# Group norm and attention over 48 x 48 images: VectorE's norm work queued instruction by instruction, another order at the start, and x buffers used for the last residuals

## The chip, the cores and the metric

The kernel runs on one core of one Trainium2 chip. The metric is the device time of one execution in microseconds (us), from ten runs of the kernel before. The engines are named as in the profile: PE (TensorE, matmuls), DVE (VectorE), ACT (ScalarE), POOL (GpSimd) and SP (SyncE, which here only issues transfers).

## The reference

Four images of 512 channels and 48 x 48 = 2304 positions ("tokens") go through a group norm, one matrix product to q, k and v, attention with 8 heads of 64 channels, and an output product that is added to the input.

```python
xr = x.reshape(b, 32, 16, h, w)                    # group norm: 32 groups of 16 channels
hn = ((xr - mean) * rsqrt(var + 1e-5)).reshape(b, c, h, w) * gn_scale + gn_bias
qkv = einsum('oc,bchw->bohw', qkv_w, hn) + qkv_b   # then cast to float16, split by head
w = softmax(einsum('bhct,bhcs->bhts', q * s, k * s))          # s = 64 ** -0.25
a = einsum('bhts,bhcs->bhct', w, v).astype(float32)
out = x + einsum('oc,bchw->bohw', proj_w, a) + proj_b
```

## The kernel before

**Tiling.** An image (a batch, b) is 512 x 2304 in channels x tokens: NC = 4 chunks of 128 channels (c), and NQ = 5 column blocks of tokens, four of 512 and one of 256 (j). So x of one batch is 20 tiles `x_b_c_j`, each with its own buffer, `x{c}_{j}`, reused from batch to batch; the norm is written over x in place. Heads are worked on in pairs, four per batch, sixteen in all (g).

**The stream.** The attention is a list of 432 *bursts*, 27 per head pair. A burst is three tiles of scores of 128 keys for both heads: six or more matmuls into PSUM (`scores`, L832), three exponentials on ACT from PSUM to an fp16 tile p (L839; three p buffers). One burst later VectorE adds p to the running sum over keys (`add`, L890, three folds at L893 at a block's end), two bursts later PE multiplies p by v into the one bank `av` (`values`, L857). At the end of a column block VectorE copies that bank out (avx, L866), and the same bank takes the sums over keys (`add_up`, sl, L910), which are copied out, sent to another layout by DMA, checked on POOL (L947), inverted on VectorE, sent through DRAM and back as a row over all partitions (ib, L966), and multiplied on POOL (att, L969).

**Fillers.** Everything else is cut into pieces in a list, `beside`, and issued between the bursts: the q and k products (`qk_chain`, L673, evacuated by VectorE at L682), the v product (`v_chain`, L713, L721), the output product (`proj_chain`, L761), whose input is converted by POOL to 32 bits (`att32`, L753) and whose result VectorE adds to a loaded piece of x (`residual`, three buffers; `proj_end`, L772), and the next batch's loads, statistics (bn_stats, L590), group mean and variance (two small matmuls, L597 and L607, with small VectorE steps and one POOL power for rstd, L615) and norm (L629). In each burst `fill` takes pieces from the head of the list as long as a credit in us allows; a piece can carry a `gap`, the least number of bursts since the last issued piece. Each run of `stats` issues four VectorE instructions (one per chunk) together, `norm` four, `group_mean` eight.

**What sets the order.** For PE and DVE the order of instructions is the order in which the code emits them. ACT, POOL and SP are placed by a scheduler. `chain_bank` gives fillers one PSUM bank at a time; the scores have three (`ps_s`), av and sl share one.

**Start and end.** At the start the x tiles of batch 0 are loaded block by block over two queues (SP and ACT), with q, k and v weights behind them; bv is spread over the partitions by POOL (`partition_broadcast`, L530); then all 20 statistics, mean, variance, and per block the norm and two chains. At the end the projection of the last batch's blocks 3 and 4 follows the last burst, and a flag (a count of sums in range, one small matmul) decides whether a general path is taken.

Of the kernel before, what the change touches and what calls it, by code (L numbers as in the profile page):

```python
# [25 lines left out]
P = 128  # L26
# [5 lines left out]
BURST = 3  # L32
# [434 lines left out]
def fast_path(  # L467
# [30 lines left out]
    def load_x(b, j, engines):  # L498

        o, n = QBLOCKS[j]  # L500
        for c in range(NC):
            t = xpool.tile([P, n], F32, tag=f"x{c}_{j}", name=f"x_{b}_{c}_{j}")
            engines[c % len(engines)].dma_start(t, x[b, bass.ts(c, P), o : o + n])
            hn[b, c, j] = t

    for j in range(NQ):
        load_x(0, j, (nc.sync, nc.scalar))
# [6 lines left out]
    brow = work.tile([1, C], F32, tag="avx", name="brow")  # L514
# [3 lines left out]
    nc.gpsimd.dma_start(bproj, proj_b)  # L518
    nc.gpsimd.dma_start(
# [3 lines left out]
    for part, engine in ((1, nc.sync), (0, nc.scalar), (2, nc.sync)):  # L523
        cols = bass.ts(part, C)
        engine.dma_start(
            wqkv[:, :, cols], qkv_wT[:, cols].rearrange("(c p) o -> p c o", p=P)
        )

    bv = const.tile([P, C], F32, name="bv")
    nc.gpsimd.partition_broadcast(bv, brow[0:1, :], P)  # L530
# [52 lines left out]
    st, mvs, coef = {}, {}, {}  # L583

    def stats(b, j):

        if j == 0:
            st[b] = small.tile([P, NC, NQ, 6], F32, tag="st", bufs=1, name=f"st_{b}")
        for c in range(NC):
            nc.vector.bn_stats(st[b][:, c, j, :], hn[b, c, j])  # L590

    def group_mean(b):
        mv = small.tile([P, NC, 2], F32, tag="mv", name=f"mv_{b}")
        for c in range(NC):
            nc.vector.bn_aggr(mv[:, c, :], st[b][:, c].rearrange("p j s -> p (j s)"))
        pm = chain_bank(f"gmean_{b}")[:, :NC]
        nc.tensor.matmul(pm, gmat2, mv[:, :, 0], start=True, stop=True)  # L597
        mean = small.tile([P, NC], F32, tag="gmean", name=f"mean_{b}")
        nc.vector.tensor_copy(mean, pm)
        dev = small.tile([P, NC], F32, tag="gdev", name=f"dev_{b}")  # L600
        nc.vector.tensor_tensor(dev, mv[:, :, 0], mean, ALU.subtract)
        dev2 = small.tile([P, NC], F32, tag="gdev2", name=f"dev2_{b}")
        nc.vector.tensor_tensor(dev2, dev, dev, ALU.mult)
        var = small.tile([P, NC], F32, tag="gvar", name=f"var_{b}")
        nc.vector.tensor_tensor(var, mv[:, :, 1], dev2, ALU.add)
        mvs[b] = mean, var

    def group_var(b):
        mean, var = mvs.pop(b)
        pv = chain_bank(f"gvar_{b}")[:, :NC]  # L610
        nc.tensor.matmul(pv, gmat2, var, start=True, stop=True)
        veps = small.tile([P, NC], F32, tag="veps", name=f"veps_{b}")
        nc.vector.tensor_scalar(veps, pv, EPS, None, ALU.add)
        rstd = small.tile([P, NC], F32, tag="rstd", name=f"rstd_{b}")
        nc.gpsimd.tensor_tensor(rstd, veps, mhalf, ALU.pow)  # L615
        ga = small.tile([P, NC], F32, tag="ga", name=f"ga_{b}")
        nc.vector.tensor_tensor(ga, rstd, gsc, ALU.mult)
        mga = small.tile([P, NC], F32, tag="mga", name=f"mga_{b}")
        nc.vector.tensor_tensor(mga, mean, ga, ALU.mult)
        gb = small.tile([P, NC], F32, tag="gb", name=f"gb_{b}")  # L620
        nc.vector.tensor_tensor(gb, gbi, mga, ALU.subtract)
        coef[b] = ga, gb

    def norm(b, j):

        ga, gb = coef[b]
        for c in range(NC):
            t = hn[b, c, j]
            nc.vector.tensor_scalar(  # L629
                t, t, ga[:, c : c + 1], gb[:, c : c + 1], ALU.mult, ALU.add  # L630
            )
# [5 lines left out]
    def piece(us, run, first=False, last=False, gap=0):  # L637
        return [us, run, first, last, gap, 0, NG]
# [20 lines left out]
    def qk_chain(g, part, j):  # L659
        b, pr = divmod(g, NPAIR)  # L660
        o, n = QBLOCKS[j]
        pw = {}

        def one(c):
# [4 lines left out]
            if c == 0:  # L669
# [557 lines left out]
```

## Time and profile before

| | |
|---|---|
| median of 10 runs | 1686.3 us (1684.07 to 1693.47) |
| profiled execution | 1691.31 us, its span 1689.5 us |
| mean granted PE clock | 0.987 |
| PE busy | 1602.8 us, 95% of the span |
| VectorE busy | 1135.1 us, 67% |
| ACT busy | 1232.6 us, 73% |
| POOL busy | 361.0 us, 21% |
| PE busy from 0 to 92 us | 65.8 us |
| PE busy from 1600 to 1690 us | 67.4 us |

The profile is of one execution. Its page gives busy time by engine, the span in 40 slices of 42.2 us (each digit the busy share in tenths, PEclk the granted clock), and the costliest groups of instructions. In the list of waits a row names the waiting instruction, the engine and instruction that released it, and after the colon the total us, how often, and the longest. In the order of time a row gives the start, the duration, the engine, the line, the operation with output <- input, and in brackets how long the engine had been idle and what ended that. In the view by windows a row gives a stretch in us, its length, the busy us of PE, PE's weight loads, DVE, ACT and POOL with their instruction counts, the granted clock, the DMA share and GB/s.

### The profile page before, as it was taken

The page shows a single profiled execution, that of the slowest core. Times are in us where ns is not written, and L with a number is a line of the kernel's source. Part 1 is how long each engine was busy: PE and PEld are TensorE (multiplying, and loading weights), DVE is VectorE, ACT ScalarE, POOL GpSimd, SP SyncE. Part 2 cuts the span into 40 slices and gives each one's busy share as a digit, 9 for nine tenths or more (in the row PEclk, how much of TensorE's full clock was granted, in tenths as well). Part 3 has the DMA queues.
Part 4 walks back from the last instruction along what each step waited for, and adds up shares of the span by engine and source line. Part 5 has one row for each costly group of instructions (what it writes and reads, how often), then busy time and mean ns, then how long its engine had stood idle before and what let it go on. Part 6 is the DMA issues. An engine that isn't in the chain of part 4 may idle for free.

```text
span 1689.5 us, 28311 instructions
## 1 busy us (share of the span) xinstructions
PE 1602.8 (95%) x11504; PEld 701.5 (42%) x11504; DVE 1135.1 (67%) x1280; ACT 1232.6 (73%) x1297; POOL 361.0 (21%) x497
## 2 busy tenths in 40 slices
PE   3999999799999999989999999999999999999795
PEld 1533454244333443445333344444533334444344
DVE  5257666876666667777666666877766666676764
ACT  0068787777887887767777877776777888877980
POOL 1002212112211211232221121133211121223331
PEclk9999999899999999999999999999999999999998
DMA  6001002200000113530200001442010000034243
GB/s 206 1 13 26 17 15 65 71 14 17 14 11 14 17 24 98 126 101 17 48 14 11 14 17 40 102 126 79 20 45 11 14 17 14 14 91 117 57 113 108
DMA packets 93772, 81.84 MB, mean 48 GB/s; under 512 B 50880, under 2 KB 58944, under 8 KB 93632
## 3 DMA queue, kind: packets, MB, share of 16 engines
q1 hardware_dynamic: 91488, 76.51, 17.3%
q10 hardware_dynamic: 1968, 3.41, 0.6%
q8 instruction: 92, 1.51, 0.4%
q14 instruction: 48, 0.39, 0.1%
q0 software_dynamic: 176, 0.02, 0.0%
HBM read 60.44 MB, written 19.16 MB: 47 GB/s over the span
## 4 chain that ended last, share of the span: by engine, by line
PE 85%; DVE 6%; DMA 3%; ACT 3%; issue 2%; POOL 0%; SPq 0%; ACTq 0%; DVEq 0%; POOLq 0%
PE pqk L673 29%; PE ps L832 17%; PE av L857 17%; PE pv L713 14%; PE pr L761 7%; ACT p L839 3%; DVE acc L890 2%; DVE st L590 1%; PE sl L910 1%; DMA out_dram<-r 1%; DVE acc L893 1%; DMA x<-x_dram 1%; DMA r<-x_dram 1%; DVE x L629 0%; DVE r L772 0%
## 5 line engine op out<-in xcount | busy, mean ns | idle before, releaser
L839 ACT ACTIVATE p<-ps 128x1024 f16<-128x1024 f32 x1296 | 1231.3, 1027 | 403.2 <-PE ps L832 401.6
L673 PE MATMUL pqk<-x,wqkv 128*64 128x512 f32 (+1 forms) x2560 | 539.3, 553 | 9.8 <-DVE x L629 5.6
L890 DVE TENSOR_TENSOR acc<-acc,p 128x3072 f16<-128x3072 f16 x270 | 487.9, 1807 | 73.7 <-ACT p L839 73.1
L832 PE MATMUL ps<-q,k 64*128 64x512 f16 (+1 forms) x2880 | 365.8, 361 | 15.6 <-ACT p L839 15.2
L857 PE MATMUL av<-p,v 128*64 128x512 f16 (+1 forms) x2880 | 364.4, 367 | 0.1
L673 PEld LDWEIGHTS pqk<-x,wqkv 128*64 128x64 f32 x2560 | 175.7, 137 | 250.2 <-issue 181.0
L947 POOL TENSOR_SCALAR in<-sums 128x8 f32<-128x8 f32 (+1 forms) x160 | 114.8, 718 | 734.4 <-DMA sums<-slx 726.9
L713 PE MATMUL pv<-wqkv,x 128*64 128x256 f32 x2304 | 267.9, 380 | 2.5 <-DVE r L772 1.5
L832 PEld LDWEIGHTS <-k 64*128 64x128 f16 x2880 | 107.7, 94 | 296.0 <-issue 250.2
L857 PEld LDWEIGHTS <-v 128*64 128x64 f16 x2880 | 132.2, 109 | 212.6 <-issue 169.5
L969 POOL TENSOR_TENSOR att<-avx,ib 128x512 f16<-128x512 f32 (+1 forms) x78 | 124.3, 1593 | 438.2 <-DMA ib<-row 376.3
L713 PEld LDWEIGHTS pv<-wqkv,x 128*64 128x64 f32 x2304 | 159.8, 137 | 96.1 <-DVE v L721 6.4
L890 DVE TENSOR_TENSOR acc<-p,p 128x3072 f16<-128x3072 f16 x80 | 140.4, 1755 | 0.3 <-ACT p L839 0.3
L761 PE MATMUL pr<-a,whi 128*128 128x512 f32 (+1 forms) x304 | 122.3, 408 | 6.1 <-POOL a L753 3.2
L682 DVE TENSOR_SCALAR q<-pqk,bqkv 128x512 f16<-128x512 f32 (+1 forms) x80 | 55.7, 696 | 100.6 <-PE pqk L673 100.3
L721 DVE TENSOR_TENSOR v<-pv,bv 128x512 f16<-128x512 f32 x72 | 49.7, 690 | 104.4 <-PE pv L713 104.3
L893 DVE TENSOR_TENSOR acc<-acc 128x1024 f16<-128x1024 f16 x156 | 112.5, 721 | 5.3
L761 PE MATMUL pr<-a,wlo 128*128 128x512 f32 (+1 forms) x304 | 114.3, 382 | 0.0
L682 DVE TENSOR_SCALAR k<-pqk,bqkv 128x512 f16<-128x512 f32 (+1 forms) x80 | 55.6, 695 | 82.9 <-PE pqk L673 82.8
L772 DVE SCALAR_TENSOR_TENSOR r<-pr,bproj,r 128x512 f32<-128x512 f32 (+1 forms) x80 | 55.3, 695 | 70.3 <-PE pr L761 57.5
L866 DVE COPY avx<-av 128x512 f32<-128x512 f32 (+1 forms) x80 | 50.8, 635 | 56.9 <-PE av L857 56.8
L753 POOL CAST a<-att 128x512 fp32r<-128x512 f16 (+1 forms) x75 | 59.3, 824 | 95.7 <-PE pr L761 95.3
(57 smaller groups left out, 423.5 us busy)
## 6 DMA issues: line engine op xcount, KB each, us to landing
r<-x_dram SPq DMA_DIRECT2D x64, 256.0 KB, 2.9
out_dram<-r SPq DMA_DIRECT2D x64, 256.0 KB, 2.5
ib<-row SPq DMA_DIRECT2D x126, 128.0 KB, 3.1
x<-x_dram SPq DMA_DIRECT2D x56, 256.0 KB, 3.7
x<-x_dram ACTq DMA_DIRECT2D x8, 256.0 KB, 6.9
wqkv<-qkv_wT_dram SPq DMA_DIRECT2D x2, 1024.0 KB, 8.1
sums<-slx SPq DMA_DIRECT2D x128, 2.0 KB, 2.1
r<-x_dram SPq DMA_DIRECT2D x16, 128.0 KB, 2.1
```

The lines of the kernel that those rows point to most:

```text
L673: nc.tensor.matmul(pw[0][lo : lo + D, :n], wqkv[:, c, w0 + lo : w0 + lo + D], hn[b, c, j], start=(c == 0), stop=(c == NC - 1),)
L682: nc.vector.tensor_scalar(qk[g][part][:, o : o + n], pw[0][:, :n], bqkv[:, col : col + 1], SCALE, ALU.add, ALU.mult,)
L713: nc.tensor.matmul(pw[0][lo : lo + D, a, :], hn[b, c, i * P // QB][:, at + lo : at + lo + D], wqkv[:, c, 2 * C + half * C // 2 :][:, : C / ...
L753: engine.tensor_copy(at32[b, j][:, c, :n], atts[b * NPAIR + c][:, o : o + n])
L761: nc.tensor.matmul(ps[:, :n], w[:, c, bass.ts(m, P)], at32[b, j][:, c, :n], start=(c == 0 and i == 0), stop=(c == NC - 1 and i == 1),)
L832: nc.tensor.matmul(ps[:, h, a * n : (a + 1) * n], kt[rows, bass.ts(i, P)], qt[rows, o : o + n], start=True, stop=True,)
L839: nc.scalar.activation(pt[:, r], ps, AF.Exp)
L857: nc.tensor.matmul(av[0][lo : lo + D, :n], vv[b, pr // 2][:, i, pr % 2 * P + lo : pr % 2 * P + lo + D], pt[:, r, h, a * n : (a + 1) * n], ...
L890: nc.vector.tensor_tensor(t, before, pt, ALU.add)
L893: nc.vector.tensor_tensor(t[:, 0], t[:, 0], t[:, r], ALU.add)
L947: nc.gpsimd.tensor_scalar(t, sm, limit, None, op)
L969: nc.gpsimd.tensor_tensor(atts[g][:, o : o + n], avx.pop((g, j))[:, :n], ib[:, :n], ALU.mult)
```

## The change

1. *Start.* x of batch 0 is loaded by channel chunk, behind the first 128 columns of the k weights; the rest of the weights follow x. Statistics, group mean, rstd and coefficients are made per chunk (`chunks` arguments), with the statistics issued two chunks ahead. The norm of batch 0 runs on ACT (`norm_chunk`). Six q and k chains are held open in the three score banks, two to a bank, and go forward chunk by chunk, with the next chunk's two small matmuls between them. The row of the v bias is written to DRAM and read back over all partitions by a DMA, in place of POOL's broadcast.
2. *Batches 1 to 3.* A reload sets its loads into a queue `loads` and its statistics as single instructions into a queue `tasks`, due three bursts later; coefficients and norms are queued the same way. In each burst `do_tasks` takes loads that are due and some tasks: 5 if the head of `beside` is not ready, none right after a block's end, 1 in the burst that sums up, else 2. `gap` goes; a piece can carry a condition `when` (the step before was issued in an earlier burst; the norm of this block is issued). Mean and rstd of these batches use a score bank (`norm_bank`), not the filler bank, and POOL's power stands where the scheduler puts it.
3. *End.* The residuals of the last batch's blocks 3 and 4 are loaded into x buffers behind its projections of blocks 0 and 1, and so are the conversions of its first three head pairs' rows (`att32`), into x buffers too; they were in the three-buffer ring, in a32 and in a p buffer.

```diff
-    def load_x(b, j, engines):
+    def load_x(b, j, c, engine):
         o, n = QBLOCKS[j]
+        t = xpool.tile([P, n], F32, tag=f"x{c}_{j}", name=f"x_{b}_{c}_{j}")
+        engine.dma_start(t, x[b, bass.ts(c, P), o : o + n])
+        hn[b, c, j] = t
+
+    def load_block(b, j):
         for c in range(NC):
-            t = xpool.tile([P, n], F32, tag=f"x{c}_{j}", name=f"x_{b}_{c}_{j}")
-            engines[c % len(engines)].dma_start(t, x[b, bass.ts(c, P), o : o + n])
-            hn[b, c, j] = t
-    for j in range(NQ):
-        load_x(0, j, (nc.sync, nc.scalar))
+            load_x(b, j, c, nc.sync)
...
-    brow = work.tile([1, C], F32, tag="avx", name="brow")
...
+    bv = const.tile([P, C], F32, name="bv")
+    brow = dram.tile([1, C], F32, tag="brow", bufs=1, name="brow")
     nc.gpsimd.dma_start(
         brow.rearrange("a (n p) -> a n p", p=P),
         qkv_b[:, 2 * NC :].rearrange("p n -> n p").unsqueeze(0),
     )
-    for part, engine in ((1, nc.sync), (0, nc.scalar), (2, nc.sync)):
-        cols = bass.ts(part, C)
+    nc.gpsimd.dma_start(bv, brow.to_broadcast((P, C)))
...
-    bv = const.tile([P, C], F32, name="bv")
-    nc.gpsimd.partition_broadcast(bv, brow[0:1, :], P)
+    load_w(1, slice(0, P), nc.scalar)
+    for c in range(NC):
+        for j in range(NQ):
+            load_x(0, j, c, nc.scalar if c == 0 and j % 2 else nc.sync)
+        if c == 0:
+            load_w(0, slice(0, P), nc.scalar)
+    load_w(1, slice(P, C), nc.sync)
+    load_w(0, slice(P, C), nc.sync)
+    load_w(2, slice(0, C), nc.sync)
...
-        pm = chain_bank(f"gmean_{b}")[:, :NC]
...
+    def group_mean(b, bank, chunks=ALL):
+        mv = stat[b][1][:, chunks[0] : chunks[-1] + 1]
+        pm = bank[:, : len(chunks)]
+        mean, dev, dev2, var = columns(b, chunks, "gmean", "gdev", "gdev2", "gvar")
         nc.tensor.matmul(pm, gmat2, mv[:, :, 0], start=True, stop=True)
...
+    def coefficients(b, chunks=ALL):
+        cs = slice(chunks[0], chunks[-1] + 1)
+        ga, mga, gb, rstd, mean = columns(
+            b, chunks, "ga", "mga", "gb", "rstd", "gmean"
+        )
+        nc.vector.tensor_tensor(ga, rstd, gsc[:, cs], ALU.mult)
         nc.vector.tensor_tensor(mga, mean, ga, ALU.mult)
...
-    def norm(b, j):
...
+    def norm(b, j, c):
+        t = hn[b, c, j]
+        ga, gb = columns(b, (c,), "ga", "gb")
+        nc.vector.tensor_scalar(t, t, ga, gb, ALU.mult, ALU.add)
+
+    def norm_chunk(b, c):
+        ga, gb = columns(b, (c,), "ga", "gb")
+        for j in range(NQ):
...
+            nc.scalar.activation(t, t, AF.Identity, bias=gb, scale=ga)
...
-    def qk_chain(g, part, j):
+    def qk_steps(g, part, j, bank=None):
         b, pr = divmod(g, NPAIR)
         o, n = QBLOCKS[j]
-        pw = {}
+        pw = {0: bank}
...
-            if c == 0:
+            if c == 0 and bank is None:
...
-        return chain_pieces(n / 600.0, one, HALVES if n == QB else WHOLE)
+        return one
...
-        xt = work.tile([P, QB], F32, tag="res", bufs=3, name=f"r_{b}_{j}_{m}")[:, :n]
+        if at_end(b, j):
+            tag = f"x{m}_{j - NQ + 2}"
+            xt = xpool.tile([P, QB], F32, tag=tag, name=f"r_{b}_{j}_{m}")[:, :n]
+        else:
+            xt = work.tile([P, QB], F32, tag="res", bufs=3, name=f"r_{b}_{j}_{m}")
+            xt = xt[:, :n]
         nc.sync.dma_start(xt, x[b, bass.ts(m, P), o : o + n])
         res[b, j, m] = xt
...
+    def at_end(b, j):
+        return b == B - 1 and j >= NQ - 2
...
         o, n = QBLOCKS[j]
-        if (b, j) == (B - 1, NQ - 1):
-            if (b, j) not in at32:
-                t = ppool.tile([P, BURST, 2, QB], F16, tag="p", name="a32_last")
-                t = t.rearrange("p r h n -> p (r h n)")[:, : 2 * NC * n]
-                at32[b, j] = t.bitcast(F32R).rearrange("p (c n) -> p c n", c=NC)
-        else:
-            at32[b, j] = work.tile(
-                [P, NC, QB], F32R, tag="a32", bufs=1, name=f"a32_{b}_{j}"
-            )
+        if (b, j) not in at32:
+            if at_end(b, j):
+                at32[b, j] = [
+                    xpool.tile([P, n], F32R, tag=f"x{c}_{j}", name=f"a32_{b}_{j}_{c}")
+                    for c in range(NC)
+                ]
+            else:
+                t = work.tile(
+                    [P, NC, QB], F32R, tag="a32", bufs=1, name=f"a32_{b}_{j}"
+                )
+                at32[b, j] = [t[:, c, :n] for c in range(NC)]
         for c in pairs:
             engine = nc.vector if direct(b * NPAIR + c, j) else nc.gpsimd
-            engine.tensor_copy(
-                at32[b, j][:, c, :n], atts[b * NPAIR + c][:, o : o + n]
-            )
+            engine.tensor_copy(at32[b, j][c], atts[b * NPAIR + c][:, o : o + n])
...
         def ahead(k):
-            if k < NQ * NC:
+            if k < NQ * NC and not at_end(b, k // NC):
...
-        convert = [piece(0.0, lambda: att32(b, j))]
+        convert = [
+            piece(0.0, lambda: att32(b, j, (NC - 1,) if at_end(b, j) else range(NC)))
+        ]
...
+    now = [0]
+    tasks, loads = deque(), deque()
+    normed, turn = set(), {}
+
+    def reload(b, j):
+        def run():
+            load_block(b, j)
+            for c in range(NC):
+                tasks.append((now[0] + 3, lambda c=c: stats(b, j, c)))
+            if j == NQ - 1:
+                tasks.append((now[0] + 3, lambda: step(aggregate, b)))
+        loads.append((now[0] + 1, run))
+
+    def step(run, b, *args):
+        run(b, *args)
+        turn[run, b] = now[0]
+
+    def follows(run, b):
+        return lambda: turn.get((run, b), now[0]) < now[0]
+
+    def norm_bank(b):
+        return ps_s.tile([P, 2, QB], F32, tag="ps", name=f"norm_{b}")[:, 0, :]
+
+    def group_scale(b):
+        group_rstd(b, norm_bank(b))
+        tasks.append((now[0] + 1, lambda: coefficients(b)))
+        for j in range(NQ):
+            for c in range(NC):
+                def run(j=j, c=c):
+                    norm(b, j, c)
+                    normed.add((b, j, c))
+                tasks.append((now[0] + 1, run))
+
+    def do_tasks(room):
+        n = now[0]
+        while loads and loads[0][0] <= n:
+            loads.popleft()[1]()
+        while tasks and tasks[0][0] <= n and room > 0:
+            tasks.popleft()[1]()
+            room -= 1
...
-            if half == 0 and i % 4 == 2 and i // 4 + 1 < NQ:
-                put_run(norm, b, i // 4 + 1)
             g = b * NPAIR + 2 * half
...
+            pieces = v_chain(b, half, i)
+            last = (b, i * P // QB, NC - 1)
+            if half == 0:
+                pieces[0][4] = lambda last=last: last in normed
+            put(pieces, (g - 2) * per_pair + 1, g)
...
-            for j in range(NQ - 1):
+            for j in range(NQ - 2):
                 put_convert(b, j)
                 put_proj(b, j)
+                if j < 2:
+                    for m in range(NC):
+                        put_run(residual, b, NQ - 2 + j, m)
+                    put_run(att32, b, NQ - 2 + j, range(NC - 1))
+            put_convert(b, NQ - 2)
+            put_proj(b, NQ - 2)
...
-            put_run(load_x, b + 1, j, (nc.sync,))
-            if j > 1:
-                put_run(stats, b + 1, j - 2)
+            put_run(reload, b + 1, j)
+        norms = [
+            (
+                lambda b=b: step(group_mean, b + 1, norm_bank(b + 1)),
+                follows(aggregate, b + 1),
+            ),
+            (lambda b=b: group_scale(b + 1), follows(group_mean, b + 1)),
+        ]
         if b > 0:
-            put_proj(old, 0)
-            put_convert(old, 1)
-        put_run(stats, b + 1, NQ - 2, gap=2 * (b == 0))
...
+            put_run(norms[0][0], when=norms[0][1])
+            put_proj(old, 3, 1)
+            put_run(norms[1][0], when=norms[1][1])
+            put_proj(old, 3, 2, 3)
...
+    six = [(1, j) for j in range(NQ)] + [(0, 0)]
+    banks = [
+        ps_s.tile([P, 2, QB], F32, tag="ps", name=f"ps_{i}") for i in range(3)
+    ]
+    chains = [qk_steps(0, *a, banks[i // 2][:, i % 2, :]) for i, a in enumerate(six)]
+
+    def all_stats(c):
+        for j in range(NQ):
+            stats(0, j, c)
+        aggregate(0, (c,))
+
+    def small_bank(name):
+        return ps_w.tile([P, QB], F32, tag="pw", name=name)
+    all_stats(0)
+    group_mean(0, small_bank("mean_0"), (0,))
+    group_rstd(0, small_bank("var_0"), (0,))
+    all_stats(1)
+    for c in range(NC):
+        coefficients(0, (c,))
+        norm_chunk(0, c)
+        if c + 2 < NC:
+            all_stats(c + 2)
+        for i, chain in enumerate(chains):
+            chain(c)
+            if c + 1 < NC and i == 1:
+                group_mean(0, small_bank(f"mean_0_{c + 1}"), (c + 1,))
+            if c + 1 < NC and i == 3:
+                group_rstd(0, small_bank(f"var_0_{c + 1}"), (c + 1,))
+    for j in range(1, NQ):
+        for p in qk_chain(0, 0, j):
+            p[1]()
...
+        now[0] = n
+        idle = beside and beside[0][4] and not beside[0][4]()
+        do_tasks(5 if idle else 0 if ended(n - 1) else 1 if ended(n - BEHIND - 1) else 2)
...
-            us, _, first, last, gap, after, _ = beside[0]
-            if after > n or n < issued[0] + gap or (first and ended):
+            us, _, first, last, when, after, _ = beside[0]
+            if after > n or (first and closed) or (when and not when()):
...
+            while loads:
+                loads.popleft()[1]()
+            while tasks:
+                tasks.popleft()[1]()
...
-    att32(B - 1, NQ - 1, range(NC - 1))
```

## The prediction

> **What bounds the kernel now.** I read the busy slices first, then TensorE's waits, then the stretches round those waits in order of time.
>
> ```profile
> PE   3999999799999999989999999999999999999795
> DVE  5257666876666667777666666877766666676764
> ```
>
> TensorE (PE) is full except in the first slice, slices 8, 17–18, 27–28 and the last three. VectorE (DVE) has room on average and is near full at slice 8. So work taken from VectorE is worth nothing in general. What counts is PE's idle time, and the list of PE's waits over the span says where it is (total us, times, longest):
>
> ```profile
> PE gmean L597 <- DVE mv L595: 27.1, 4, 19.8
> PE ps L832 <- ACT p L839: 15.2, 35, 0.5
> PE sl L910 <- DVE avx L866: 11.0, 7, 4.9
> PE count L1171 <- DVE good L1169: 6.5, 1, 6.5
> PE pqk L673 <- DVE x L629: 5.6, 1, 5.6
> ```
>
> The 19.8 and the 5.6 are the start, the 6.5 is the end, and the rest lies in three stages, one per new batch, where statistics and norm of that batch pass through VectorE. Summed over stages, PE is idle 11.6 us in 300–400, 8.1 in 600–800 and 8.5 in 1000–1200: 28.2 us. One such wait in order of time (start, us, engine):
>
> ```profile
> 327.67 2.46 DVE L590 BATCH_NORM_STATS2 st<-x 128x6 f32<-128x512 f32 x4
> ...
> 330.05 0.67 DVE L866 COPY avx<-av 128x512 f32<-128x512 f32 x1
> ...
> 330.78 0.64 PE L910 MATMUL sl<-acc,ones 128*64 128x512 f16 x2 [4.89 <-DVE avx L866]
> ```
>
> Four statistics stand as a block in VectorE's queue ahead of the copy that frees PE's bank. The windows view prices what follows (PE busy, then the granted clock after the POOL column):
>
> ```profile
> 331.00:334.00 3.00, 1.81 (x8) 0.29 (x6) 3.00 (x6) 2.00 (x3) 0.00 (x0) 0.50 0.01 0
> 342.00:346.00 4.00, 3.90 (x34) 2.06 (x36) 3.19 (x6) 1.19 (x2) 2.01 (x1) 1.00 0.20 62
> ```
>
> After the stall PE runs at half clock until about 338. About 5.0 us of PE's busy time lies in that spell, so half, 2.5 us, is lost on top; likewise about 3 us behind the gmean wait at 728 and 4.5 behind those at 1112 and 1144. The stages hold 28.2 + 10 = 38 us.
>
> **The change, part by part.** The sum is made against the profiled execution, 1691.3 us with a span of 1689.5. Its 1.8 us outside the span stay. It lies 5 us above the median of 1686.3, within the ten runs, so I take the difference off the median.
>
> **Start.** Before, GpSimd (POOL) sets it:
>
> ```profile
> 13.90 0.80 POOL L530 PARTITION_BROADCAST bv<-brow  x1 [7.88 <-issue]
> 14.56 0.46 POOL L553 TENSOR_SCALAR_AFFINE_SELECT gmat<-gmat 128x128 f32<-128x128 f32 x1
> 25.08 1.05 POOL L615 TENSOR_TENSOR rstd<-veps,mhalf 128x4 f32<-128x4 f32 x1 [10.06 <-issue]
> ```
>
> rstd's input was ready at 22.0, yet it ran at 25.08: POOL was held about 10 us after the broadcast instruction, which the change removes. The first chain starts at 27.36. Now bv comes by a DMA from DRAM, and in POOL's built order the second half of gmat stands behind that DMA's issue, which waits for brow to land. brow took 8.4 us from 3.81, so 12.2; plus an issue (0.55 to 1.15 here) and 0.46, gmat is ready at about 13.5. Chunk 0's statistics (five tiles, landing by about 8) are done by then. From 13.5: mean matmul 0.56, four small VectorE steps 0.8, variance matmul 0.6, veps 0.2, pow 1.05: 16.8. But VectorE's next instructions are chunk 1's statistics (4 x 0.69 + 0.4, plus aggregate, 3.2 us, to 19.0), and only then the coefficients (0.5). ScalarE's norm of 128x512 is not in the trace; below, VectorE's 0.54, above, the exp of twice the elements at 1.03; I take 0.6, as half of exp plus some fixed part. PE starts at about 20.1, 7.3 us earlier.
>
> It gives most of that back. Before, 27.36 to 60.28 was one unbroken 32.9 us. Now each chunk has five and a half chain steps of 0.86 (4.7 us), two small matmuls inside (0.3 each in the stream, bound above by their isolated 0.56), and a gap: after the variance matmul come veps 0.2, pow 1.05, coefficients 0.5, norm 0.6 and handovers, 2.5 us, against 1.3 us of chains left. Three gaps of 1.2 and six matmuls of 0.3 add 5.4. Net gain **2 us** (from -2, if brow's write to DRAM lands 2 us later and the matmuls cost 0.56, to +4). Here a rule speaks against it: the Trainium skill, "TensorE: Matmul & The Clock Gate" (the table "Why this matters for your kernels"), wants no idle gaps above about 3 us and about 4 us of continuous work to reach full clock. Rows: a 2.71 us gap at 1656 was followed by a clock of 0.52, a 0.73 gap at 1663.8 by 1.00, and the 0.5 us gaps at 320–325 by 1.00. By rule and rows 1.2 us keeps the clock; if it did not, four chunks at half clock cost 4 x 4.7 less the 1.9 paid today, 17 us.
>
> **Stage 1 (300–400).** In the built order two of the four statistics of column block 2 now stand ahead of the accumulations and those of block 1 a burst or more earlier, so the fold ends near 325.3, not 327.7. The four statistics of block 3 (2.46) still stand before the avx copy: sl at 328.4, not 330.8. That is 2.4 us of idle gone and perhaps the cold spell. The gmean wait (2.2) goes, since its matmul comes a burst later. Against it, six bursts run without filler instead of five. Followed to the end of the first pv chain: before 345.8; now acc_2_4 ends at 340.0, coefficients and first norm 341.0, chain end 344.7, with one burst more behind it (scores and values, 1.55). Gain **2.6**.
>
> **Stage 2 (600–800).** Goes: 8.1 idle and 3 half clock. Left: about 1.5 of small evacuation waits and 0.6 of matmuls. New: rstd now stands behind att<-avx_1 on POOL. That product needs an ib row, which came 6.0 to 9.8 us after its reciprocal in this trace (337.98 to 343.99; 707.78 to 717.59), takes 2.2 to 2.6, and rstd 1.05. VectorE reaches the coefficients about 8.0 us after the same reciprocal, so it is held 1.9 to 5.4 us with every evacuation and accumulation queued behind. PE has a burst of slack: 0 to 3.7 lost. The longer path is the nearer one, since residual and output DMAs share SP's queue here as there; I take 3.7. Gain 11.1 - 5.8, **5**.
>
> **Stage 3 (1000–1200).** 8.5 and 4.5 go; POOL's conversions (2.4 of waits, 1.3 of cold clock) and 0.6 of matmuls stay; rstd stands behind nothing late. Gain 8.7; I take **8**.
>
> **The price of spreading.** A burst with a PE filler takes 3.59 us. With two tasks VectorE needs 1.75 (accumulate) + 0.75 (evacuate) + 1.31 (two statistics; norms 1.08) = 3.81, 0.22 too much. Some 20 such bursts per batch, partly caught at block ends, which get none or one: about 1 us per batch, **-3**.
>
> **End.** Before, PE is done at 1675.7 and the end waits for residuals cycling through three buffers:
>
> ```profile
> 1675.41 0.27 PE L761 MATMUL pr<-a_last,wlo 128*128 128x256 f32 x1
> ...
> 1681.55 0.48 DVE L772 SCALAR_TENSOR_TENSOR r<-pr,bproj,r 128x256 f32<-128x256 f32 x1 [0.95 <-DMA r<-x_dram]
> ```
>
> Eight residual loads and six POOL casts move some 30 bursts forward. SP issues the loads at 0.33 each, behind PE's release of x; POOL is 21% busy and its casts stand after x is free in the built order. PE then only waits for one cast (0.81, hidden behind six matmuls): pr_3 from 1662.9 to 1670.7, pr_4 3.9 to 1674.6, two evacuations and the count to 1676.1, against 1682.5. Gain **6.4**. The 7 us behind the flag stay.
>
> Sum: 2 + 2.6 + 5 + 8 - 3 + 6.4 = 21. Profiled execution 1670; median 1686.3 - 21 = **1665**.
>
> **Rivals.**
> - *The waits only change places*: VectorE's order is fuller, so PE waits for evacuations what it waited for gmean. For: VectorE over 90% busy in 310–330. Against: no block of four remains in stages 2 and 3. Only start and end count: 8.4, giving 1678.
> - *More is gained*: all idle and half clock of the stages goes but 5 us: 33 + 8.4, giving 1645. Against: the rstd order.
> - *The gate stays half shut at the start*: 21 - 17, giving 1682.
> - *Slower*: accumulation beside a busy POOL is not 1.75 but 2.2 (321.54: two in 4.47), so a two-task burst takes 4.3, 0.7 too much, and three p buffers and one projection bank pass all of it to PE. 60 bursts x 0.7 = 42, less the 21 + 3 already counted: 18 slower, 1704. It decides from 0.4 us per burst on. Against: most accumulations show 1.75.
> - *Not what it says*: the built order shows the parts in place, so hardly.
>
> **Numbers.** Forecast 0.55 (1655–1674), change of places 0.18, more 0.09, gate 0.05, slower 0.13. Faster by over 0.2% (3.4 us, about what a measurement of this kernel can tell from no change): 0.83; within: 0.04 (half of the gate case and some of the change of places); slower: 0.13. The range 1652–1683 leaves out the slower case and most of the better one.
>
> **What would show it.** First chain near 20, its end near 58; no sl wait above 3 us and no gmean wait in the stages; a wait of VectorE's ga for rstd of 2 to 5 us in stage 2; the end about 7 us after the last projection matmul instead of 14. It is wrong if PE's waits for evacuations or ps grow by more than 20 us, or the clock in the stages falls below today's.

## The result, and the profile after

The changed kernel takes 1678.3 us (median of 15 runs, 1674.3 to 1683.2) against 1686.3 before: ratio 0.9952, interval 0.9942 to 0.9962. That is 8 us faster where 21 were forecast; it lies inside the stated range (1652 to 1683).

The busy slices of the changed kernel's page (a slice is now 41.9 us):

```profile
PE   3999999989999999989999999999999999999896
DVE  3247666887666767867666666787766666666774
```

The dent at slice 8 is shallower (8 for 7), the one near slice 18 is as it was, and the end is fuller (896 for 795). The first slice is as empty as before. The list of PE's waits over the span (total us, times, longest):

```profile
PE mean L622 <- POOL gmat L565: 19.3, 1, 19.3
PE ps L871 <- ACT p L878: 14.8, 34, 0.5
PE pr L798 <- POOL a L792: 7.7, 5, 4.6
PE ps L696 <- ACT x L654: 7.2, 4, 4.5
PE sl L949 <- DVE avx L905: 6.8, 4, 2.7
PE pv L741 <- DVE x L647: 4.3, 4, 1.7
PE ps L696 <- DVE k L705: 2.7, 3, 0.9
PE count L1292 <- DVE good L1290: 1.0, 1, 1.0
```

The group means of the three stages have gone from the list, sl fell from 11.0 to 6.8, and the end's wait from 6.5 to 1.0. New are the wait of the first small matmul for gmat (a constant matrix that POOL fills), the waits of the open chains for ScalarE's norm and for their own evacuations, and 4.6 us for one of POOL's conversions.

**Where the time went.** The start of each burst's first exponential on ACT is a clock for the whole stream: between two stages (bursts 90 to 144 and 207 to 261) its distances agree to 0.01 us from kernel to kernel. The kernel before was profiled a second time, in an execution of 1686.43 us (span 1684.6), which is its median. Expected were a start of 89.4 to 91 us and stages within 1.5 us of the first profile; so came the start and two stages, but the third was 2.6 us shorter. The first exponential of the changed kernel, and of the second profile before:

```profile
100.41 2.85 ACT L878 ACTIVATE p<-ps 128x1024 f16<-128x1024 f32 x3 [49.21 <-PE ps L871]
90.21 2.86 ACT L839 ACTIVATE p<-ps 128x1024 f16<-128x1024 f32 x3 [73.01 <-PE ps L832]
```

The account of that second profile against the changed kernel's (span 1675.0):

| part | forecast | before, second profile | after | gain |
|---|---|---|---|---|
| start, to the first exponential | +2 | 90.21 | 100.41 | -10.2 |
| stage 1, bursts 54 to 90 | +2.6 | 135.55 | 132.16 | +3.4 |
| stage 2, bursts 144 to 207 | +5 | 238.51 | 238.87 | -0.4 |
| stage 3, bursts 261 to 333 | +8 | 274.55 | 265.19 | +9.4 |
| spreading | -3 | | | in the stages |
| end, from the last exponential | +6.4 | 37.7 | 30.4 | +7.3 |
| sum | 21 | 1684.6 | 1675.0 | +9.6 |

The three stages with their price of spreading were forecast at 12.6 and brought 12.4, partly by luck: stage 2 missed by 5.4, and the other two stages (+0.8, +1.4) and the price that was not paid (+3) made up for it. Each row is one pair of profiles, and stage 2 is the least certain: it took 239.0 and 239.1 in two other kernels whose order there is the changed kernel's (tasks_only and start_old below), but 241.3 to 242.4 in three more (bv_evac, brow_late, bv_sync), whose engines all have the changed kernel's order of instructions behind the start. The end brought one more than forecast. The start took back 10.

### The profile page after: what moved, and what is told of

Same layout as the page of the kernel before. It is cut to its first block, busy times and chain, and to the rows that moved or that the text cites. A ratio compares the mean times of both kernels' runs of the same rounds, so it can differ in the third digit from the quotient of the medians.

```text
span 1675.0 us, 28357 instructions
## 1 busy us (share of the span) xinstructions
PE 1599.3 (95%) x11516; PEld 700.3 (42%) x11516; DVE 1130.2 (67%) x1284; ACT 1246.5 (74%) x1317; POOL 362.0 (22%) x500
## 4 chain that ended last, share of the span: by engine, by line
PE 88%; DVE 3%; ACT 3%; DMA 2%; POOL 1%; issue 1%; SPq 0%; POOLq 0%; DVEq 0%; ACTq 0%
PE pqk L696 29%; PE ps L871 17%; PE av L896 17%; PE pv L741 15%; PE pr L798 7%; ACT p L878 3%; DVE acc L929 1%; PE sl L949 1%; PE ps L696 1%; DMA brow<-qkv_b_dram 1%; POOL a L792 1%; DMA ib<-row 1%; DVE r L809 0%; DVE st L605 0%; DMA r<-x_dram 0%
## 5 line engine op out<-in xcount | busy, mean ns | idle before, releaser
L696 PE MATMUL pqk<-x,wqkv 128*64 128x512 f32 (+1 forms) x2464 | 518.2, 551 | 1.8 <-DVE r L809 0.9
L986 POOL TENSOR_SCALAR in<-sums 128x8 f32<-128x8 f32 (+1 forms) x160 | 110.4, 690 | 722.8 <-DMA sums<-slx 715.0
L696 PEld LDWEIGHTS pqk<-x,wqkv 128*64 128x64 f32 x2464 | 168.8, 137 | 228.1 <-issue 171.8
L705 DVE TENSOR_SCALAR k<-pqk,bqkv 128x512 f16<-128x512 f32 (+1 forms) x75 | 52.2, 696 | 78.0 <-PE pqk L696 77.7
L792 POOL CAST a<-att 128x512 fp32r<-128x512 f16 (+1 forms) x78 | 68.1, 905 | 93.2 <-PE pr L798 92.4
```

The source lines that it names most:

```text
L696: nc.tensor.matmul(pw[0][lo : lo + D, :n], wqkv[:, c, w0 + lo : w0 + lo + D], hn[b, c, j], start=(c == 0), stop=(c == NC - 1),)
L705: nc.vector.tensor_scalar(qk[g][part][:, o : o + n], pw[0][:, :n], bqkv[:, col : col + 1], SCALE, ALU.add, ALU.mult,)
L792: engine.tensor_copy(at32[b, j][c], atts[b * NPAIR + c][:, o : o + n])
L986: nc.gpsimd.tensor_scalar(t, sm, limit, None, op)
```

## The experiments

Every kernel below is the changed kernel with the edit shown, unless it says otherwise. Ratios are to the kernel before, run on the same chip.

| kernel | time, us | ratio (interval) | first exponential |
|---|---|---|---|
| changed kernel | 1678.3 | 0.9952 (0.9942-0.9962) | 100.4 |
| start_old | 1672.3 | 0.9908 (0.9892-0.9925) | 89.4 |
| tasks_only | 1675.6 | 0.9934 (0.9918-0.9951) | 90.5 |
| bv_sync | 1676.2 | 0.9929 (0.9913-0.9945) | 97.6 |
| bv_evac | 1671.5 | 0.9902 (0.9886-0.9918) | 93.2 |
| brow_late | 1668.2 | 0.9890 (0.9870-0.9910) | 90.0 |
| div_late | 1675.8 | 0.9930 (0.9913-0.9947) | 101.3 |
| early_only | 1677.0 | 0.9948 (0.9930-0.9965) | 100.8 |
| late_evac_div | 1660.6 | 0.9849 (0.9831-0.9868) | 86.9 |
| all_early | 1654.3 | 0.9806 (0.9789-0.9824) | 86.8 |
| stats_after | 1654.3 | 0.9816 (0.9797-0.9834) | 84.9 |
| old_late | 1659.1 | 0.9829 (0.9807-0.9851) | 87.3 |

### Which part loses: start_old and tasks_only

start_old puts the start of the kernel before back (loads by column block, POOL's broadcast, VectorE's norm, ten chains in a row).

```diff
-    load_w(1, slice(0, P), nc.scalar)
-    for c in range(NC):
-        for j in range(NQ):
-            load_x(0, j, c, nc.scalar if c == 0 and j % 2 else nc.sync)
+    for j in range(NQ):
+        for c in range(NC):
+            load_x(0, j, c, (nc.sync, nc.scalar)[c % 2])
...
+    nc.gpsimd.partition_broadcast(bv, brow[0:1, :], P)
```

> The changed kernel with the old start: x by column block on two queues, the bias spread by POOL, all statistics first, VectorE's norm per block, ten chains one after the other; its tasks and its end stay. Theory 1 (the new start costs 8.5 us, and nothing behind it absorbs them): the first exponential comes back from 100.4 to about 91.9 us, bursts 0 to 54 keep their distances, and the time falls from 1678.3 to about 1670. Rival (the stream has slack that swallows a later start, or the two profiles compared are not typical): within 3 us of 1678.

The first exponential came at 89.4 and the time fell by 0.44% (7.4 us; the two intervals together allow some 3 either way). So the new start loses 7 to 11 us. Some of the 11 that the first exponential shows was not in the total: the two executions differ by 0.8 us in stage 1 and by 2.0 us behind the flag.

tasks_only goes back at the end too (`at_end` returns False, and the residuals and conversions are as before).

> The changed kernel with both the old start and the old end: the tasks of batches 1 to 3 alone. By the two profiles the three stages bring 14 us and the end 8, by the medians start_old left 15 for both together. Theory (the end is worth its 8, since it is the same in every execution, and the stages bring the rest, 7): about 1680, against before's 1687. Rival (the stages bring 12 or more, the end little): about 1675.

1675.6 is the rival's time. By the ratios the stages alone bring 0.66% (11 us) and the end 0.26%, 4 us with 4 either way. The profiles of start_old and tasks_only differ by more, 8.4 us in span, 6.9 of it behind the last exponential. The forecast of 12.6 for the stages holds; the expectation's 7 for them was too low.

### Why the start loses: bv_sync, brow_late, bv_evac

The bias row `brow` goes to DRAM and comes back over all partitions as `bv`. POOL's rows in the order of time, changed kernel:

```profile
3.67 1.15 POOL L522 DMA_DIRECT2D brow<-qkv_b_dram  x1
...
18.35 0.57 POOL L526 DMA_DIRECT2D bv<-brow  x1 [12.73 <-DMA brow<-qkv_b_dram]
18.94 0.34 POOL L565 TENSOR_SCALAR_AFFINE_SELECT gmat<-gmat 128x128 f32<-128x128 f32 x1
```

The prediction saw this order, and put the landing at 12.2. It was 18.1: the 512 pieces of 4 bytes took 8.4 us to a row in SBUF in the kernel before, and 14.4 to DRAM here. bv_sync issues the read-back from SP, behind the weights.

```diff
-    nc.gpsimd.dma_start(bv, brow.to_broadcast((P, C)))
...
     load_w(2, slice(0, C), nc.sync)
+    nc.sync.dma_start(bv, brow.to_broadcast((P, C)))
```

> The changed kernel, but the read-back of the bias row over the partitions is issued by SP behind the weights, not by POOL ahead of the second half of gmat. Theory 1 (of the start's loss, the larger part is gmat held by the bias row's landing): the second half of gmat runs at about 6 us instead of 18.94, the first chain's matmul at about 16.5 instead of 25.89, the first exponential at about 91 instead of 100.4, the time about 1669. Rival (the start is bound by x's arrival or by VectorE's statistics of chunk 1 as well): the first chain not before 21, gain 4 us or less.

gmat was whole at 6.1, yet the first chain came at 22.35 and the gain was 4 us: the rival. What it waited for stands in VectorE's rows (bv_sync):

```profile
11.76 0.68 DVE L605 BATCH_NORM_STATS2 st<-x 128x6 f32<-128x512 f32 x1
18.51 2.20 DVE L605 BATCH_NORM_STATS2 st<-x 128x6 f32<-128x512 f32 x4 [6.06 <-DMA x<-x_dram]
20.75 0.29 DVE L610 BATCH_NORM_AGGREGATE mv<-st 128x2 f32<-128x30 f32 x1
20.95 0.10 DVE L640 TENSOR_TENSOR ga<-rstd,gsc 128x1 f32<-128x1 f32 x1
```

"Statistics two chunks ahead" puts chunk 1's statistics ahead of chunk 0's coefficients, and chunk 1's x was not there. Eight x tiles that SP had issued from 5.2 to 10.0 in the changed kernel landed from 18.3 on (not ten, as the expectation below has it), right behind the bias row. SP issued no further x tile from 10.0 to 18.3 either; it waited for an earlier one to land. brow_late moves the row's first transfer behind the weights as well.

```diff
-    nc.gpsimd.dma_start(
-        brow.rearrange("a (n p) -> a n p", p=P),
-        qkv_b[:, 2 * NC :].rearrange("p n -> n p").unsqueeze(0),
-    )
...
     load_w(2, slice(0, C), nc.sync)
+    nc.sync.dma_start(
+        brow.rearrange("a (n p) -> a n p", p=P),
+        qkv_b[:, 2 * NC :].rearrange("p n -> n p").unsqueeze(0),
+    )
```

> The changed kernel, but both transfers of the bias row (its write to DRAM in 512 pieces of 4 bytes, and its read-back) are issued by SP behind x and the weights. Theory 1b (the row's write, which landed at 18.1 us, also holds up the x tiles: ten of them issued from 5.2 to 10.0 us landed only from 18.3 to 24 us, and with bv_sync VectorE waited for chunk 1's until 18.5): the x tiles of chunk 1 land by about 12 us, the last by 18 instead of 28, the first chain's matmul comes at about 16.5, the first exponential at about 91.5 (bv_sync 97.6), the time about 6 us below bv_sync's 1676, 1670. Rival (chunk 1 is late because SP can only have so many transfers under way): x lands as in bv_sync, same time within 2 us.

Measured: first chain 15.95, 6.6 us below bv_sync by the ratios. The DMA view of the first 40 us, in slices of 1 us, shows the cause. The changed kernel:

```profile
GB/s 0 35 142 334 404 340 360 288 162 222 277 209 64 14 14 10 41 121 123 123 303 288 298 307 375 395 388 379 370 373 378 381 387 391 387 225 27 0 0 0
```

and brow_late:

```profile
GB/s 0 29 114 322 400 354 362 293 307 383 382 378 387 381 379 385 381 371 372 373 376 380 387 348 43 10 0 0 37 20 43 27 35 29 20 45 371 291 123 0
```

With the 2 KB row in front, the 16 engines move 10 to 64 GB/s from 12 to 16 us, with most of x still to come. Without it they stay near 380 until x and weights are in at 25; x is complete at 18.2 instead of 28. A hole as deep now stands behind that, from 24 to 36: the row and the weights of the output product, issued behind it from 16.6 on, land at 34 to 38, and nobody needs them yet. The rival is out: SP's wait for earlier x tiles shrinks with the hole (9.9 us in all in the changed kernel, 2.7 here).

The Trainium skill, "DMA: Bandwidth & Descriptors" (section "Issuing engines are not separate DMA queues"), says that transfers of all issuing engines run on the same 16 DMA engines. That fits: POOL's small transfer held SP's large ones, and SP's own small transfer held SP's. What counted was the row's place in time. Is it the piece size or the writing to DRAM? The kernel before, with the same pieces to SBUF, has a hole too, but a smaller one:

```profile
GB/s 0 33 135 391 393 393 359 300 338 125 126 246 393 383 393 367 351 345 397 387 399 387 391 385 389 383 387 94 0 0 0 0 0 0 0 0 0 8 0 0
```

There the x tile that SP issued at 4.6 landed at 12.2, with the row; in old_late (below), with the row behind the weights, one issued at 4.4 landed at 10.3. So these small pieces hold other transfers also when they go to SBUF. Whether the deeper hole here comes from DRAM as the destination or from the other order of the loads, no run took apart.

bv_evac adds to bv_sync another order at the end of the chunk pass. The six open chains lie two to a score bank (one tile), and in the last chunk PE (time, us, idle before) did this in the changed kernel:

```profile
48.65 1.08 PE L696 MATMUL ps<-x,wqkv 128*64 128x512 f32 x4 [0.87 <-ACT x L654]
50.67 1.94 PE L696 MATMUL ps<-x,wqkv 128*64 128x512 f32 x8 [0.95 <-DVE k L705]
53.55 1.51 PE L696 MATMUL ps<-x,wqkv 128*64 128x512 f32 x8 [0.94 <-DVE k L705]
55.86 1.08 PE L696 MATMUL ps<-x,wqkv 128*64 128x512 f32 x4 [0.81 <-DVE k L705]
```

```diff
-            chain(c)
+            chain(c, close=False)
+            if c == NC - 1 and i % 2:
+                chains[i - 1].finish()
+                chain.finish()
```

> As bv_sync, and in the last channel chunk the two chains that share a score bank are both finished by PE before either is evacuated. Theory (PE's three waits of 0.9 us at 49.8 to 55.9 come from writing one half of a bank whose other half VectorE has to read first, not from a lack of evacuations): these three waits go, 2.7 us less than bv_sync, about 1666. Rival (the next pair of chains waits for the evacuations anyway): same as bv_sync within 1 us.

The same stretch in bv_evac is one row, 24 matmuls without a wait:

```profile
44.76 4.94 PE L696 MATMUL ps<-x,wqkv 128*64 128x512 f32 x24 [0.86 <-ACT x L654]
```

The second chain of a bank had waited until VectorE had read the first one's half; whether the program's order or the memory asks for that wait was not tried. The first exponential came 4.5 us earlier, and the time fell by 0.27% (4.5 us, with some 4 either way) where 2.7 were expected. The three waits are not the whole price: the last chunk's 24 matmuls take 8.12 us from first start to the next chain in the changed kernel and 4.77 here, so 3.4. In bv_sync, moreover, eight of these matmuls ran at 0.4 us each (3.24 us from 46.59), under a granted clock of 0.57 from 46.6 to 50. That came in none of the other eight profiles with this start.

### Why stage 2 gains nothing: div_late, early_only, all_early

POOL's rows of the changed kernel in stage 2, then PE's:

```profile
713.49 0.61 POOL L792 CAST a<-att 128x512 fp32r<-128x512 f16 x1 [3.03 <-PE pr L798]
718.37 1.26 POOL L1008 TENSOR_TENSOR att<-avx,ib 128x512 f16<-128x512 f32 x1 [4.27 <-DMA ib<-row]
719.57 1.72 POOL L792 CAST a<-att 128x512 fp32r<-128x512 f16 x3
```

```profile
720.24 0.80 PE L798 MATMUL pr<-a,whi 128*128 128x512 f32 x1 [4.63 <-POOL a L792]
```

The multiply att waits for its row from DRAM, with three of four conversions behind it, and PE waits for these. Then PE runs at 0.63 us a matmul instead of 0.40 (granted clock 0.50 from 720.2 to 723). That burst took 9.97 us. In the kernel before, the four conversions stood together ahead of att, and the burst took 3.59:

```profile
709.48 2.29 POOL L753 CAST a<-att 128x512 fp32r<-128x512 f16 x4 [0.64 <-PE pr L761]
717.59 2.61 POOL L969 TENSOR_TENSOR att<-avx,ib 128x512 f16<-128x512 f32 x1 [5.82 <-DMA ib<-row]
```

div_late issues the fillers of a burst ahead of the division, which turns this one order on POOL.

```diff
-        if ended(n - BEHIND - 3):
-            divide(*stream[n - BEHIND - 3][:2])
         if not summed:
             fill(n)
+        if ended(n - BEHIND - 3):
+            divide(*stream[n - BEHIND - 3][:2])
```

> The changed kernel with one order turned in each burst: the fillers are issued ahead of the division by the sums. In POOL's queue this moves one multiply, att of batch 1 (second norm stage), from between the first and the other three casts of one conversion to behind them. Theory 2 (that multiply waits for its row from DRAM with three casts behind it, PE waits 4.6 us for the casts and runs cold after it, and this is why the second stage gains nothing): the 9.97 us burst falls to about 3.6, the time by 6 to 8, to about 1671. Rival (PE would wait there for the bank or the row anyway, so the wait changes place): less than 2 us.

The burst fell to 4.67, but the time only by 0.22% (3.7 us, with some 3 either way): a miss by half. By profile stage 2 got 2.9 us shorter, 5.3 in this burst less 2.4 in others. Of VectorE's waits this one is larger in div_late (second row) than in the changed kernel (first row):

```profile
DVE ga L640 <- POOL rstd L633: 2.2, 1, 2.2
DVE ga L640 <- POOL rstd L633: 3.6, 1, 3.6
```

and PE pays for it (div_late, in the order of time; r is an evacuation that stands behind ga on VectorE):

```profile
747.04 0.50 PE L798 MATMUL pr<-a,whi 128*128 128x512 f32 x1 [2.32 <-DVE r L809]
```

It looks as if the wait for rstd took what the casts freed. The traces do not show that. brow_late, whose order in stage 2 is the changed kernel's, has the same wait:

```profile
DVE ga L640 <- POOL rstd L633: 3.7, 1, 3.7
```

In four other kernels of that order it is 2.2 to 2.5, and in late_evac_div below, with the order turned, 2.8. On POOL the att ahead of this rstd waited 7.7 us for its row in brow_late and in div_late, and 6.0 in the changed kernel; so the size goes with the landing of the row. early_only undoes rstd's place behind att alone, by issuing mean and rstd of batches 2 and 3 one projection chain earlier.

```diff
-            put_proj(old, 3, 0)
             put_run(norms[0][0], when=norms[0][1])
-            put_proj(old, 3, 1)
+            put_proj(old, 3, 0)
             put_run(norms[1][0], when=norms[1][1])
-            put_proj(old, 3, 2, 3)
+            put_proj(old, 3, 1, 2, 3)
```

> The changed kernel with only the mean and the rstd of batches 2 and 3 put one projection chain earlier (the cast order of the second stage stays as it is, with att between one cast and three). Theory (in the changed kernel VectorE waits 2.2 us for rstd behind att in the second stage; PE's part of it is what the prediction called 0 to 3.7): VectorE's wait goes, the stage from burst 175 to 198 gets 2 to 4 us shorter, the time falls to about 1675. Rival (it counts only once the casts are in order, since PE's own wait for the casts has already put VectorE behind): less than 1 us.

The time stayed within 0.7 us (with some 3 either way), which is the rival's size, but the profile does not bear out its reason. VectorE's wait fell to 0.9, and bursts 175 to 198 took 85.6 us instead of 87.8: the gain that the theory expected is there. It was lost ahead of them, where bursts 172 and 173 took 15.8 us instead of 13.5. VectorE stood there for the sums of a block, which came late by DMA (early_only):

```profile
712.12 0.20 DVE L993 RECIPROCAL inv<-sums 128x8 f32<-128x8 f32 x1 [3.62 <-DMA sums<-slx]
```

bv_sync and bv_evac, with the changed kernel's order there, show that wait too (3.8 and 3.7), and 16.6 and 15.7 us for these two bursts. So it comes without early_only's edit too, and the time does not decide between theory and rival. late_evac_div (brow_late, bv_evac and div_late together) and all_early (early_only's edit on top) tell what both are worth:

> brow_late with bv_evac's order of evacuations at the start and div_late's order of fillers and division. Theory (three independent losses, so their sizes add): 3 to 4.5 us below brow_late by the evacuations, and 3 to 4 by the division: about 1664. Rival (they are not additive, since what one frees the next wait takes): not below 1668.

> late_evac_div with the mean and the rstd of batches 2 and 3 put one projection chain earlier in the list of fillers; in POOL's queue this moves the second stage's rstd ahead of att, as it was in the kernel before. Theory 2b (in div_late VectorE waited 3.6 us for rstd behind att, and PE 2.3 us for the evacuation behind that wait): VectorE's wait for rstd in the second stage falls below 1.2 us, PE's wait goes, the time falls by 2 to 3, to about 1662. Rival (the burst of slack covers it, or the wait comes back elsewhere): within 1 us of late_evac_div.

late_evac_div took 1660.6, 7.5 below brow_late: the losses add, and the rival is out. all_early took 1654.3, by the ratios 7 us less where 2 to 3 were expected; the two profiles differ by 4.1. Stage 2 took 237.7 and then 232.3 us. Of these 5.4 us, 2.7 lie in bursts 175 to 181, where rstd's place acts, as expected; 2.4 lie in bursts 172 and 173, where late_evac_div's profile shows the late sums again (3.5). Why the medians differ by more is open. The changed kernel took 238.9 in this stage and the kernel before 238.5.

### What is left of the start by chunks: stats_after, old_late

stats_after is all_early with chunk 1's statistics behind chunk 0's coefficients.

```diff
-    all_stats(1)
     for c in range(NC):
         coefficients(0, (c,))
         norm_chunk(0, c)
+        if c == 0:
+            all_stats(1)
```

> all_early with the statistics of chunk 1 at the start issued behind the coefficients and the norm of chunk 0, not ahead of them. Theory (these 3.0 us of statistics stand in VectorE's queue between chunk 0's rstd, ready at 12.6, and its coefficients at 14.9, and nothing else holds the first chain): first chain's matmul 2.2 us earlier, at about 14.2, first exponential at about 84.7, time about 1652. Rival (chunk 1's mean is then late, and the gap moves between chunks 0 and 1): first chain earlier, but the first exponential within 1 us of 86.8.

First chain 14.14, first exponential 84.9, as expected; the median is all_early's, and the intervals overlap, so no gain in time is shown. old_late replaces the start of stats_after by the old one, with the bias row behind the weights.

> The best version so far (stats_after) with the old start by column blocks in place of the one by channel chunks, but with the bias row's two transfers behind the weights there too, so that neither start has POOL's broadcast or the held x tiles; division and norm order as in all_early. What is the start by chunks worth once its faults are mended? Theory (chunks start PE about 10 us earlier, at 14.1, and pay some 7 us of gaps and small matmuls, so little is left): x complete by 16.5, first chain at about 23.5, first exponential at about 87.5 against 84.9, time about 1657. Rival (the old start mended is as good, since PE's unbroken pass is the shorter one): 1654 or less.

First exponential 87.3 and 1659.1 us, near the theory's sizes. By profile the mended chunk start leads by 2.4 us; the ratios (0.9829 and 0.9816) don't tell them apart. The best versions, all_early and stats_after, are both near 1654, some 1.9% faster than the kernel before.

## Why the prediction was wrong, step by step

- **Start, +2 forecast, -10.2 measured: the step that failed.** Three terms. (1) "brow took 8.4 us from 3.81, so 12.2": that row was of a transfer to SBUF; the new one writes DRAM and took 14.4. The first matmul, which needs gmat, came at 19.3, where gmat was forecast for 13.5. The range allowed 2 us for it, and 5.8 were needed. That x itself is held by the row was not thought of; here the later gmat hid it, since chunk 1's x was in at 19.3 and VectorE came to its statistics at 21.5. (2) "Three gaps of 1.2 and six matmuls of 0.3 add 5.4" to a pass of 32.9. From first chain to first v product it took 42.9, 4.6 more than that: 3.4 for the two halves of a bank in the last chunk, which the sum leaves out, 0.9 in the first chunk and 0.4 in the next two (6.7 us each, forecast 6.5). The slow first matmuls are no part of it, since the 32.9 holds them too (before, then the changed kernel):

```profile
27.36 3.68 PE L673 MATMUL pqk<-x,wqkv 128*64 128x512 f32 x8 [5.56 <-DVE x L629]
25.89 3.68 PE L696 MATMUL ps<-x,wqkv 128*64 128x512 f32 x8 [4.54 <-ACT x L654]
```

(3) The 27.36 it started from was high: POOL's hold before rstd was 10.1 us in that profile and 8.4 to 9.7 in three others with that start, where the first chain came at 25.3 to 26.5. Against the second profile before this is worth 1.7 at the first exponential. 5.8, 4.6 and 1.7 make the miss of 12. The weighing of the clock rule was right for this kernel, whose granted clock stays 1.00 through the pass with gaps of 0.9 us; bv_sync's 0.57 shows that such gaps do not always keep it.
- **Stage 1, +2.6, measured +3.4: right.** The longest wait of sl is 2.7 (before 4.9), and the gmean waits are gone.
- **Stage 2, +5, measured -0.4: wrong, the second step that failed.** "rstd now stands behind att<-avx_1" was right in kind and in VectorE's wait: 2.2 us of the 1.9 to 5.4 forecast. By early_only's profile it cost PE about 2.2 of the 3.7 charged. But POOL's order was searched for rstd alone. Three conversions behind another att, 27 us earlier, were put at nothing and were the larger loss (4.6 us of PE's idle time, and a burst of 9.97 us that took 3.59 before). The rival that waits change places came true for this stage only, and with a wait for POOL, not for VectorE's evacuations.
- **Stage 3, +8, measured +9.4: right.** The first profile would have given 12.0: 2.6 us of that execution's losses there did not come back in the second.
- **Spreading, -3: not there.** Of stage 3's bursts with a piece of the output product and two statistics, two took 3.58 and 3.65 us, as such bursts do without; a third took 4.61, with PE waiting 0.72 for a conversion. VectorE's rows of the one of 3.65, up to the next accumulation (changed kernel, stage 3):

```profile
1104.72 1.75 DVE L929 TENSOR_TENSOR acc<-acc,p 128x3072 f16<-128x3072 f16 x1
1106.38 0.20 DVE L993 RECIPROCAL inv<-sums 128x8 f32<-128x8 f32 x1
1106.50 1.23 DVE L605 BATCH_NORM_STATS2 st<-x 128x6 f32<-128x512 f32 x2
1108.05 0.75 DVE L809 SCALAR_TENSOR_TENSOR r<-pr,bproj,r 128x512 f32<-128x512 f32 x1 [0.32 <-PE pr L798]
1108.72 2.14 DVE L929 TENSOR_TENSOR acc<-acc,p 128x3072 f16<-128x3072 f16 x1
```

The sum of durations said 3.81, 0.22 too much. But from start to start the accumulation takes 1.66, not 1.75, the evacuation 0.67, not 0.75, and VectorE even has 0.32 to spare. Durations overlap by about 0.08 us. This fits the Trainium skill, "Perfetto Trace Analysis" (section "Summary: the profiler window per engine type"), which has VectorE's window reach to the acknowledgement of the last write; no run here shows that part of a row by itself. The *slower* rival did not come about either: after the 2.14 us accumulation of the last row VectorE still stood idle for 0.93 us before its next evacuation, though 0.72 of it goes with PE's wait for the conversion, so little of it was to spare.
- **End, +6.4, measured +7.3: right.** The last evacuations end 0.9 us behind PE's last projection matmul, without a wait for a residual:

```profile
1666.42 0.27 PE L798 MATMUL pr<-a,wlo 128*128 128x256 f32 x1
1666.73 0.88 DVE L809 SCALAR_TENSOR_TENSOR r<-pr,bproj,r 128x256 f32<-128x256 f32 x2 [1.02 <-PE pr L798]
...
1667.73 0.19 PE L1292 MATMUL count<-ones,good 128*1 128x1 f32 x2 [1.04 <-DVE good L1290]
```

The direction and the end were right, and the stages in sum with the luck told above. The start decided the size, most of all its term for the bias row: without that row in front (brow_late) the first exponential comes at 90.0 instead of 100.4. (The second small matmul of the norm stands in line 611 of the kernel before; the description above gives another line for it.)

## What to carry to other kernels

Don't price a moved transfer by a row with another destination, and look at what is queued behind it: a 2 KB row in 4-byte pieces held up x for some 10 us, and cost the start nothing once it stood behind what the start needs. When an order on an engine changes, list every neighbour of an instruction that waits for a DMA, not only the instruction that one came to look for. VectorE's budget in a burst is made from starts to starts, not from durations; and what a single profile shows, a start or a wait for a DMA, should be seen in a second one before its microseconds are spent or a cause is read from them.

## What was not expected of the hardware

- The write of 512 pieces of 4 bytes to DRAM took 14.4 us from POOL. From SP its read-back could be issued only 18.5 us behind it (15.7 to 34.2, brow_late), some 9 us of that after the weights ahead of it had landed (25.0). During it all transfers together fell to between 10 and 64 GB/s (changed kernel, 12 to 16 us), where they run near 380 without it (brow_late).
- PE's first matmuls of the chains took 0.46 us each (eight in 3.68, before and after) under a granted clock shown as 1.00, and 0.24 from some 6 us on in the changed kernel. The granted clock doesn't show this slow beginning, though it shows the half clock after later stalls (0.50 at 720.2).
